# A selective-scan block on one core: delta*u stored twice and spread from sixteen rows, partitions in another order, two buffers for y

## The chip, the core and the metric

The kernel runs on one NeuronCore of a Trainium2 chip; the other cores are idle. The metric is the device time of one launch in microseconds (us). A core has five engines that run side by side and wait for each other through semaphores: PE (matmul), DVE (vector), ACT (activation), POOL (GpSimd) and SP, which here does nothing but issue DMA transfers. A transfer is cut into packets that run on up to 16 DMA engines[...].

## The reference, cut to what matters

Layer 0 is a residual block with a selective scan over 4 directions; layer 1 is linear attention and a feed-forward net in reduced precision. The change touches the scan and what feeds it.

```python
# xs: B=8 images, 4 directions k, 192 channels d, L = 64*64 positions
x_dbl = einsum('bkdl,kcd->bkcl', xs, x_proj_w)          # 6 + 16 + 16 rows
dts, Bs, Cs = split(x_dbl, [6, 22], axis=2)
delta = softplus(einsum('bkrl,kdr->bkdl', dts, dt_proj_w) + dt_proj_b)
A = -exp(A_log)                                         # 192 channels x 16 states
# for every position in turn:
h = exp(delta*A) * h + (delta*u) * B                    # [b, k, d, 16 states]
y = sum over states of h * C,  plus D*u
# then: sum of the 4 directions, layernorm, gate silu(z), projection, residual
x = x + ...
t = x + attention(layernorm(x));  t = t + ffn(layernorm(t))
```

## The kernel before, in words

The 8 images go through in 4 pairs, one pair after the other, and each pair through five stages: `front` (norms, input projection, depthwise convolution), `prepare`, `scan`, `back` (sum of the directions, norm, gate, projection) and `tail` (attention and feed-forward). Within `prepare`, `front`, `back` and `tail` the framework places the instructions; `scan` stands under `tc.manual_schedule()`, so that its instructions stand on each engine in the order in which the Python loop issues them. Every DMA of the kernel is issued on SP, in one queue. Eight semaphores are used for the DMAs in turn, so an issue can also wait until the transfer eight places ahead has landed.

`prepare` computes, per direction k and chunk of 512 positions, the rows B and C (L332 to L334, stored to the scratch tensors `bs` and `cs_`), delta (L341), and delta*u (L345). `spread` (L292) stores delta*u to the scratch tensor `du` (float32, pieces of 512 bytes) and delta, cut into three bf16 parts, to `dl` (pieces of 256 bytes).

`scan` works on 128 steps per pair: 4 directions times 32 time chunks of 128 positions (TC). The 128 partitions hold 16 states n and 8 slots s, where a slot is one of the 2 images b and one of 4 blocks of 48 channels; partition p = 8 n + s. The 48 channels of a block are walked in 4 rounds r of 12 channels (NI). Per step there are 8 half rounds v, two for each r:

- `fetch` (L432) loads `dut`: delta*u of one round, the same for all 16 states. It is one DMA of 128 rows of 6144 bytes, the source being 8 rows of `du` and a leading broadcast of 16:

```python
du[k, c, :, g % 4].rearrange("s i t -> s (i t)").unsqueeze(0).to_broadcast([NS, 8, NI * TC])
```

- `load` (L403) loads `dm`, delta in its three parts, for two rounds: 24 rows of 6144 bytes, each to 3 partitions. `decay` (L473) multiplies it on PE with `aw` (which holds A for each partition) and ACT takes the exponential (L491) in PSUM tile `da`.
- `drive` (L451): ACT copies the state carried over from the step before (L463), and POOL multiplies `dut` with B, tile `bt` (L466), into `dbu`.
- `run` (L493): DVE scans 6 channels times 128 positions (L501) from `da` and `dbu` into `h`.
- `sums` (L506): PE multiplies `h` with C, tile `cw` (L519), and ACT takes the result from PSUM to `yev` (L524). `yev` holds two steps and has one buffer; `store` (L529) writes it to `ys` after every second step with 4 DMAs, at v = 6.

`load_bc` (L416) is a generator that loads B and C for 4 steps at once: 4 DMAs for `bt` (32 partitions each, partitions j, j+4, ...), then 8 for `cw` (16 partitions each). `next(more)` (L556) issues one of these DMAs per v. Before the first step 4 of the 12 are issued (L545). `dut` has 4 buffers, `dm` 3, `bt`, `dbu` and `h` 2, `da` 3 and `yp` 2.

At the head of the kernel L91 to L101 load the projection weights with the two images' state columns interleaved, and L148 to L160 write the masked A to `awd` in the order (state, slot).

Of the kernel before, what the change touches and what calls it, by code (L numbers as in the profile page):

```python
# [10 lines left out]
F32 = mybir.dt.float32  # L11
# [25 lines left out]
W6 = 6 * SEG  # L37
HQ = TC // 4
LOGEXP = "natural_log_exp_and_others"

# [7 lines left out]
def vss_attn_ffn(ctx: ExitStack, tc: tile.TileContext, a: dict):  # L50
# [37 lines left out]

    xw = const.tile([128, KD, 3, 76], F32, name="xw")
    dtw = const.tile([128, KD, 3, 128], F32, name="dtw")  # L90
    with tc.tile_pool(name="xprep", bufs=2) as wp:  # L91
        for k in range(KD):
            for g in range(2):
                xg = wp.tile([128, 3, 2 * NS], F32, name="xg")
                nc.sync.dma_start(xg, a["xw"][k, :, g, :, 0:32])
                for b in range(2):
                    nc.vector.tensor_copy(
                        xw[:, k, :, 32 * g + b : 32 * g + 32 : 2], xg[:, :, NS * b : NS * b + NS]
                    )
            nc.sync.dma_start(xw[:, k, :, 64:76], a["xw"][k, :, 0, :, 32:44])  # L100
            nc.sync.dma_start(dtw[64:76, k], a["dtw"][k])  # L101

    def cut(name, v, *rest):

# [25 lines left out]
    with tc.tile_pool(name="aprep", bufs=1) as wp:  # L130
        am = wp.tile([128, KD, 2, NS], F32, name="am")
        nc.sync.dma_start(am, a["alog"])
        nc.scalar.activation(am, am, AF.Exp)
        nc.vector.tensor_scalar(am, am, -1.0, None, ALU.mult)
        for i in range(3):
            ap = wp.tile([128, KD, 2, NS], BF16, name=f"ap{i}")
            nc.vector.tensor_copy(ap, am)
            if i < 2:
                nc.vector.tensor_tensor(am, am, ap, ALU.subtract)
            for k in range(KD):  # L140
                nc.sync.dma_start(ad[i, k, 0:128], ap[:, k, 0])
                nc.sync.dma_start(ad[i, k, 128:DI], ap[0:64, k, 1])
        mask = wp.tile([72, 8], F32, name="mask")
        for p in range(3):
            nc.sync.dma_start(
                mask[24 * p : 24 * p + 24], ident[0:8, 0:8].unsqueeze(1).to_broadcast([8, 3, 8])
            )
        for k in range(KD):  # L148
            ac = wp.tile([72, 48 * NS], BF16, name="ac", bufs=2)
            for i in range(6):  # L150
                nc.sync.dma_start(
                    ac[12 * i : 12 * i + 12],
                    ad[:, k].rearrange("a (s c) n -> s a (c n)", s=4),
                )
            aw = wp.tile([72, 48 * NS, 8], BF16, name="awp", bufs=2)
            nc.vector.tensor_tensor(
                aw, ac.unsqueeze(2).to_broadcast([72, 48 * NS, 8]),
                mask.unsqueeze(1).to_broadcast([72, 48 * NS, 8]), ALU.mult,
            )
            nc.sync.dma_start(awd[k], aw.rearrange("p c m -> p (c m)"))  # L160


    w1q = const.tile([DIM, HID], F8, name="w1q")
# [137 lines left out]
    def prepare(xi, us, dl, du, bs, cs_):  # L301
        with ExitStack() as st:
            tmp = st.enter_context(tc.tile_pool(name="p2", bufs=3))
            ps = st.enter_context(tc.tile_pool(name="p2ps", bufs=3, space=PSUM))
            pd = st.enter_context(tc.tile_pool(name="p2pd", bufs=4, space=PSUM))

            for T in range(3):
                spread(lambda o, n: us[o : o + n], T, xi[T])
            dlv = dl.rearrange("k c a s r i t -> k c a (s r i) t")
            duv = du.rearrange("k c s r i t -> k c (s r i) t")  # L310
            for o in range(2):
                for c in range(NCH):
                    cs = bass.ts(c, F)
                    if o == 0:
                        u = [t[:, cs] for t in xi]
                    else:
                        u = []
                        for T in range(3):
                            ut = tmp.tile([128, F], F32, name=f"u{T}", bufs=2)
                            nc.gpsimd.tensor_copy(  # L320
                                ut.rearrange("p (w h) -> p w h", h=HH),
                                xi[T].rearrange("p (h w) -> p w h", w=HH)[:, bass.ts(c, ROWS), :],
                            )
                            u.append(ut)
                    for k in (o, o + 2):
                        pt = ps.tile([128, F], F32, name="pt")
                        for T in range(3):
                            nc.tensor.matmul(
                                pt[:76], xw[:, k, T], u[T], start=(T == 0), stop=(T == 2)
                            )  # L330
                        S = tmp.tile([128, F], F32, name="S")
                        nc.scalar.activation(S[:76], pt[:76], AF.Copy)  # L332
                        nc.sync.dma_start(bs[k, :, cs], S[0:32])
                        nc.sync.dma_start(cs_[k, :, cs], S[32:64])  # L334
                        for T in range(3):
                            pq = pd.tile([128, F], F32, name="pq")
                            nc.tensor.matmul(  # L337
                                pq, dtw[64:76, k, T], S[64:76], start=True, stop=True
                            )
                            d = tmp.tile([128, F], F32, name="delta")  # L340
                            nc.scalar.activation(  # L341
                                d, pq, AF.Softplus, bias=dtb[:, k, half(T) : half(T) + 1]
                            )
                            q = tmp.tile([128, F], F32, name="du")
                            nc.vector.tensor_tensor(q, d, u[T], ALU.mult)  # L345
                            j = slice(c * F // TC, (c + 1) * F // TC)
                            spread(
                                lambda o, n: duv[k, j, o : o + n].rearrange("j p t -> p j t"),
                                T, q.rearrange("p (j t) -> p j t", t=TC),
                            )  # L350

                            dp = tmp.tile([128, F // TC, 3, TC], BF16, name="dp")
                            rest = tmp.tile([128, F], F32, name="rest")
                            d, rest = [
                                t.rearrange("p (j t) -> p j t", t=TC) for t in (d, rest)
                            ]
                            nc.scalar.activation(dp[:, :, 0], d, AF.Copy)  # L357
                            nc.vector.tensor_tensor(rest, d, dp[:, :, 0], ALU.subtract)  # L358
                            nc.scalar.activation(dp[:, :, 1], rest, AF.Copy)  # L359
                            nc.gpsimd.tensor_tensor(dp[:, :, 2], rest, dp[:, :, 1], ALU.subtract)  # L360
                            spread(
                                lambda o, n: dlv[k, j, :, o : o + n]
                                .rearrange("j a p t -> p (j a) t"),
                                T, dp.rearrange("p j a t -> p (j a) t"),
                            )
            nc.scalar.preload_act_table_set(LOGEXP)


    def scan(dl, du, bs, cs_, ys):
        with ExitStack() as st:  # L370
# [45 lines left out]
            def load_bc(s):  # L416
# [6 lines left out]
                i = s // NB  # L423
                bt[i] = wk.tile([128, NB * TC], F32, name="bt")
                for j in range(4):
                    nc.sync.dma_start(bt[i][j::4], bs[k, :, ts])
                    yield
                for m in range(8):
                    nc.sync.dma_start(cw[i % 2][m::8, m, :], cs_[k, m // 4 :: 2, ts])
                    yield  # L430

            def fetch(g):  # L432
                if g >= 4 * N:
                    return
                k, c, _ = steps[g // 4]
                dut[g] = ring.tile([128, NI, TC], F32, name="dut")
                nc.sync.dma_start(
                    dut[g],
                    du[k, c, :, g % 4].rearrange("s i t -> s (i t)").unsqueeze(0)
                    .to_broadcast([NS, 8, NI * TC]),  # L440
                )

            def segs(t, back):
# [62 lines left out]
            def sums(s, f):  # L506

                if f == 0:
                    yev[s] = (
                        yev.pop(s - 1) if s % 2  # L510
                        else one.tile([128, 2, HQ, 48], F32, name="yev")
                    )
                h = hs[s][:, 1:, :].rearrange("p (i u) r -> p i u r", u=SEG)
                y = yp[f % 2]
# [27 lines left out]
            load(0)  # L542
            fetch(0)
            more = load_bc(0)
            for _ in range(4):  # L545
                next(more)
            for g in range(1, 3):
                load(g)
# [222 lines left out]
    for pair in range(npair):  # L771
        zs = dram.tile([2, 2, DIM, L], F32, name="zs")
        us = dram.tile([2 * DI, L], F32, name="us")
        dl = dram.tile([KD, NT, 3, 8, NR, NI, TC], BF16, name="dl")
        du = dram.tile([KD, NT, 8, NR, NI, TC], F32, name="du")
        bs = dram.tile([KD, 2 * NS, L], F32, name="bs")
        cs_ = dram.tile([KD, 2 * NS, L], F32, name="cs")
        ys = dram.tile([KD, 8, L, 48], F32, name="ys")
# [126 lines left out]
```

## Time and profile before

| what | us |
|---|---|
| median of 3 runs | 16007.57 (15930.12 to 16009.15) |
| the profiled execution, its own time | 16024.39 |
| its span, first to last instruction | 16022.1 |
| DVE scans L501, 4096 of 1758 ns | 7021.7 busy |
| POOL products L466, 2048 of 3445 ns | 7040.6 busy |
| ACT exponentials L491, 4096 of 798 ns | 3254.2 busy |
| PE matmuls L485 and L519 | 3242.8 and 3000.8 busy |

In the profile PE is a matmul, PEld a weight load, SPq the DMA-issuing queue. L466 is line 466 of the kernel. "busy" sums the durations of a group, "idle before" is the time in which the engine stood still just before an instruction of the group, with the releaser that ended it. The row DMA gives the mean busy share of the 16 DMA engines. A pair takes about 4000 us: the first scan instruction of the first pair stands at 748.3 us, and the second pair's first load at 4030 us.

### The profile page before, as it was taken

The numbers are of one execution on the slowest core, as the hardware profiler recorded it, in microseconds if no ns is written. First come the engines' busy times: TensorE is split into PE (matmuls) and PEld (weight loads), VectorE is DVE, ScalarE is ACT, GpSimd is POOL, SyncE is SP. The second block draws the span as 40 slices with busy tenths as digits, with TensorE's granted clock in tenths as the row PEclk, the third lists the DMA queues.
The fourth block names the chain that finished last, engine by engine and source line by source line (L and its number), as shares of the span: only waits on it lengthen the run. The fifth ranks groups of instructions, "written<-read, shape, count | busy, mean of one in ns | idle before, by whom it ended". The sixth has DMA issues, their size and how long they took to land. (4 is left out here: it accounts for less than half of the span.)

```text
span 16022.1 us, 390169 instructions
## 1 busy us (share of the span) xinstructions
PE 10317.2 (64%) x171008; PEld 6805.4 (42%) x171008; DVE 8452.8 (53%) x6351; ACT 6748.1 (42%) x11498; POOL 7760.5 (48%) x2682
## 2 busy tenths in 40 slices
PE   7755555567875555557787555555678755555577
PEld 2244444443324444444332444444533244444453
DVE  1466666642146666663214666666421466666632
ACT  2544444435354444443535444444353544444435
POOL 0466666620046666662004666666200466666620
PEclk9655555576865555557686555555778655555576
DMA  1999999971189999997119999999711999999971
GB/s 48 210 220 217 214 218 212 213 160 35 39 204 218 220 217 217 221 217 153 29 42 211 218 215 215 210 214 217 157 33 41 212 216 218 222 218 216 214 152 27
DMA packets 1903136, 2784.10 MB, mean 174 GB/s; under 512 B 1254372, under 2 KB 1451861, under 8 KB 1898837
## 3 DMA queue, kind: packets, MB, share of 16 engines
q1 hardware_dynamic: 1901428, 2759.13, 74.3%
q8 instruction: 1341, 21.97, 0.7%
q14 instruction: 367, 3.00, 0.1%
HBM read 2322.98 MB, written 435.63 MB: 172 GB/s over the span
## 5 line engine op out<-in xcount | busy, mean ns | idle before, releaser
L501 DVE TENSOR_TENSOR_SCAN h<-da,dbu 128x774 f32<-128x774 f32 x4096 | 7021.7, 1758 | 3454.8 <-POOL dbu L466 3364.1
L466 POOL TENSOR_TENSOR dbu<-dut,bt 128x1536 f32<-128x1536 f32 x2048 | 7040.6, 3445 | 3449.7 <-ACT dbu L463 1841.8
L485 PE MATMUL da<-dm,aw 72*128 72x128 bf16 (+2 forms) x28672 | 3242.8, 279 | 3868.9 <-DVE h L501 3522.9
L491 ACT ACTIVATE da<-da 128x768 f32<-128x768 f32 x4096 | 3254.2, 798 | 3503.1 <-PE da L485 3497.7
L485 PEld LDWEIGHTS <-aw 72*128 72x128 bf16 x28672 | 2500.7, 130 | 4452.9 <-issue 4364.7
L519 PE MATMUL yp<-h,cw 128*8 128x48 f32 x131072 | 3000.8, 272 | 752.5 <-issue 673.9
L519 PEld LDWEIGHTS yp<-h,cw 128*8 128x8 f32 x131072 | 2487.0, 122 | 1201.5 <-issue 1051.2
L524 ACT ACTIVATE yev<-yp 128x384 f32<-128x384 f32 x2048 | 1003.3, 490 | 2620.0 <-PE yp L519 1463.5
L320 POOL COPY u<-xi 128x512 f32<-128x512 f32 x96 | 111.4, 1175 | 1505.0 <-PE pc L283 1474.2
L360 POOL TENSOR_TENSOR dp<-rest,dp 128x512 bf16<-128x512 f32 x384 | 462.2, 1204 | 710.8 <-ACT dp L359 690.3
L283 PE MATMUL pc<-y,diag 128*128 128x512 f32 x1728 | 742.3, 592 | 0.0
L690 POOL MEMSET tn<- 1x4096 f32 x8 | 27.8, 3506 | 1384.4 <-DVE t L660 1384.4
L345 DVE TENSOR_TENSOR du<-delta,xi 128x512 f32<-128x512 f32 x192 | 131.9, 687 | 1066.7 <-ACT delta L341 779.7
L337 PE MATMUL pq<-S,dtw 12*128 12x512 f32 x768 | 580.8, 860 | 129.1 <-ACT delta L341 74.7
L358 DVE TENSOR_TENSOR rest<-delta,dp 128x512 f32<-128x512 f32 x384 | 302.5, 789 | 663.8 <-ACT dp L357 663.8
L760 POOL TENSOR_TENSOR ot<-t,y 96x512 f32<-96x512 f32 x64 | 73.5, 1149 | 1176.7 <-DVE y L758 1161.7
L623 PEld LDWEIGHTS py<-ident,yk 128*96 128x96 f32 x4096 | 521.3, 178 | 226.7 <-issue 192.0
L623 PE MATMUL py<-ident,yk 128*96 128x128 f32 x4096 | 544.5, 291 | 95.7 <-DMA yk<-ys 92.8
L283 PEld LDWEIGHTS pc<-y,diag 128*128 128x128 f32 x1728 | 326.4, 189 | 415.4 <-issue 415.4
L638 ACT ACTIVATE sq<-yc 96x512 f32<-96x512 f32 x128 | 75.9, 593 | 987.2 <-PE yc L635 882.7
L463 ACT COPY dbu<-h 128x12 f32<-128x12 f32 x1984 | 413.8, 209 | 37.4 <-DVE h L501 20.7
L337 PEld LDWEIGHTS pq<-S,dtw 12*128 12x128 f32 x768 | 156.5, 243 | 547.9 <-ACT delta L341 182.3
(125 smaller groups left out, 6894.5 us busy)
## 6 DMA issues: line engine op xcount, KB each, us to landing
dut<-du SPq DMA_DIRECT2D x2048, 768.0 KB
dm<-dl SPq DMA_DIRECT2D x1024, 432.0 KB
dl<-dp SPq DMA_DIRECT2D x256, 384.0 KB
ys<-yev SPq DMA_DIRECT2D x1024, 96.0 KB
du<-du SPq DMA_DIRECT2D x256, 256.0 KB
dl<-dp SPq DMA_DIRECT2D x256, 192.0 KB
yk<-ys SPq DMA_DIRECT2D x512, 96.0 KB
yk<-ys SPq DMA_DIRECT2D x1024, 48.0 KB
```

Of the source, the lines that this page charges most:

```text
L283: nc.tensor.matmul(pc, diag[:, half(T), t, :], pad[T][:, r0 + dy : r0 + dy + ROWS, dx : dx + HH], start=(t == 0), stop=(t == 8),)
L337: nc.tensor.matmul(pq, dtw[64:76, k, T], S[64:76], start=True, stop=True)
L358: nc.vector.tensor_tensor(rest, d, dp[:, :, 0], ALU.subtract)
L360: nc.gpsimd.tensor_tensor(dp[:, :, 2], rest, dp[:, :, 1], ALU.subtract)
L463: nc.scalar.copy(start, times(hs[s - 1][:, :, r])[:, :, 0 if back else TC - 1])
L466: nc.gpsimd.tensor_tensor(times(t), dut.pop(g), bt[s // NB][:, bass.ts(c % NB, TC)].unsqueeze(1) .to_broadcast([128, NI, TC]), ALU.mult,)
L485: nc.tensor.matmul(t[:, x0:x1], aw[k, r][:, 6 * hf + e, :], dm[p // 4][:, NI * (r % 2) + 6 * hf + e, x0 - lo : x1 - lo], start=True, stop= ...
L491: nc.scalar.activation(e, e, AF.Exp)
L501: nc.vector.tensor_tensor_scan(hs[s][:, w, r][:, d], da[p % 3][:, o : o + W6][:, d], dbu[4 * s + r][:, w][:, d], 0.0, ALU.mult, ALU.add,)
L519: nc.tensor.matmul(y[32 * q : 32 * q + 8, 48 * j : 48 * j + 48] .rearrange("p (r i) -> p i r", r=NR), cw[s // NB % 2][:, :, tb], h[:, :, t ...
L524: nc.scalar.activation(yev[s][:, steps[s][1] % 2, 8 * f : 8 * f + 8, :].rearrange("p j e -> p (j e)"), y[:, 0 : 8 * 48], AF.Copy,)
L623: nc.tensor.matmul(o, yk[:, k, j, g * DIM : (g + 1) * DIM], ident, start=(k + j == 0), stop=(k + j == KD + 2),)
```

## The change

delta*u is stored twice, to `du[k, c, v]` with v = 0 and 1. `fetch` reads 16 rows, (v s), each broadcast to 8 neighbouring partitions, in place of 8 rows under a broadcast of 16. The partitions are now ordered (half of the states v, slot s, state within the half): p = 64 v + 8 s + n. `bt` and `cw` follow: `bt` is filled by 4 DMAs of 32 partitions, each from 8 rows under a leading broadcast of 4; `cw` by 16 DMAs of 8 partitions in place of 8 of 16. 12 of the now 20 loads of `load_bc` are issued before the first step. `awd` is written in the new order, and the projection weights are loaded straight into their tile, without the interleaving copies on DVE. `yev` is taken from the pool with two buffers.

```diff
-    with tc.tile_pool(name="xprep", bufs=2) as wp:
-        for k in range(KD):
-            for g in range(2):
-                xg = wp.tile([128, 3, 2 * NS], F32, name="xg")
-                nc.sync.dma_start(xg, a["xw"][k, :, g, :, 0:32])
-                for b in range(2):
-                    nc.vector.tensor_copy(
-                        xw[:, k, :, 32 * g + b : 32 * g + 32 : 2], xg[:, :, NS * b : NS * b + NS]
-                    )
-            nc.sync.dma_start(xw[:, k, :, 64:76], a["xw"][k, :, 0, :, 32:44])
-            nc.sync.dma_start(dtw[64:76, k], a["dtw"][k])
+    for k in range(KD):
+        nc.sync.dma_start(xw[:, k, :, 0:32], a["xw"][k, :, 0, :, 0:32])
+        nc.sync.dma_start(xw[:, k, :, 32:64], a["xw"][k, :, 1, :, 0:32])
+        nc.sync.dma_start(xw[:, k, :, 64:76], a["xw"][k, :, 0, :, 32:44])
+        nc.sync.dma_start(dtw[64:76, k], a["dtw"][k])
...
-            aw = wp.tile([72, 48 * NS, 8], BF16, name="awp", bufs=2)
+            aw = wp.tile([72, 96, 8, 8], BF16, name="awp", bufs=2)
             nc.vector.tensor_tensor(
-                aw, ac.unsqueeze(2).to_broadcast([72, 48 * NS, 8]),
-                mask.unsqueeze(1).to_broadcast([72, 48 * NS, 8]), ALU.mult,
+                aw,
+                ac.rearrange("p (c n) -> p c n", n=8).unsqueeze(2).to_broadcast([72, 96, 8, 8]),
+                mask.unsqueeze(2).unsqueeze(1).to_broadcast([72, 96, 8, 8]), ALU.mult,
             )
...
-            duv = du.rearrange("k c s r i t -> k c (s r i) t")
+            duv = du.rearrange("k c v s r i t -> k c v (s r i) t")
...
-                            spread(
-                                lambda o, n: duv[k, j, o : o + n].rearrange("j p t -> p j t"),
-                                T, q.rearrange("p (j t) -> p j t", t=TC),
-                            )
+                            for v in range(2):
+                                spread(
+                                    lambda o, n: duv[k, j, v, o : o + n]
+                                    .rearrange("j p t -> p j t"),
+                                    T, q.rearrange("p (j t) -> p j t", t=TC),
+                                )
...
                 for j in range(4):
-                    nc.sync.dma_start(bt[i][j::4], bs[k, :, ts])
+                    v, b = divmod(j, 2)
+                    n0 = NS * b + 8 * v
+                    nc.sync.dma_start(
+                        bt[i][32 * j : 32 * j + 32],
+                        bs[k, n0 : n0 + 8, ts].unsqueeze(0).to_broadcast([4, 8, NB * TC]),
+                    )
                     yield
                 for m in range(8):
-                    nc.sync.dma_start(cw[i % 2][m::8, m, :], cs_[k, m // 4 :: 2, ts])
-                    yield
+                    for v in range(2):
+                        p0, n0 = 64 * v + 8 * m, NS * (m // 4) + 8 * v
+                        nc.sync.dma_start(
+                            cw[i % 2][p0 : p0 + 8, m, :], cs_[k, n0 : n0 + 8, ts]
+                        )
+                        yield
...
-                    du[k, c, :, g % 4].rearrange("s i t -> s (i t)").unsqueeze(0)
-                    .to_broadcast([NS, 8, NI * TC]),
+                    du[k, c, :, :, g % 4].rearrange("v s i t -> (v s) (i t)").unsqueeze(1)
+                    .to_broadcast([16, 8, NI * TC]),
...
-                        else one.tile([128, 2, HQ, 48], F32, name="yev")
+                        else wk.tile([128, 2, HQ, 48], F32, name="yev")
...
-            for _ in range(4):
+            for _ in range(12):
                 next(more)
...
-        du = dram.tile([KD, NT, 8, NR, NI, TC], F32, name="du")
+        du = dram.tile([KD, NT, 2, 8, NR, NI, TC], F32, name="du")
```

More of the change, by code (lines that the diff above doesn't have):

```diff
@@ L154, in vss_attn_ffn @@
                 )
-            aw = wp.tile([72, 48 * NS, 8], BF16, name="awp", bufs=2)
+            aw = wp.tile([72, 96, 8, 8], BF16, name="awp", bufs=2)
             nc.vector.tensor_tensor(
-                aw, ac.unsqueeze(2).to_broadcast([72, 48 * NS, 8]),
-                mask.unsqueeze(1).to_broadcast([72, 48 * NS, 8]), ALU.mult,
+                aw,
+                ac.rearrange("p (c n) -> p c n", n=8).unsqueeze(2).to_broadcast([72, 96, 8, 8]),
+                mask.unsqueeze(2).unsqueeze(1).to_broadcast([72, 96, 8, 8]), ALU.mult,
             )
-            nc.sync.dma_start(awd[k], aw.rearrange("p c m -> p (c m)"))
+            nc.sync.dma_start(awd[k], aw.rearrange("p c m n -> p (c m n)"))
     w1q = const.tile([DIM, HID], F8, name="w1q")
```

## The prediction

> **What bounds the kernel now.** I read the page first: span, slices, queues, costliest groups.
>
> ```profile
> span 16022.1 us, 390169 instructions
> ...
> DMA  1999999971189999997119999999711999999971
> GB/s 48 210 220 217 214 218 212 213 160 35 39 204 218 220 217 217 221 217 153 29 42 211 218 215 215 210 214 217 157 33 41 212 216 218 222 218 216 214 152 27
> ...
> L501 DVE TENSOR_TENSOR_SCAN h<-da,dbu 128x774 f32<-128x774 f32 x4096 | 7021.7, 1758 | 3454.8 <-POOL dbu L466 3364.1
> L466 POOL TENSOR_TENSOR dbu<-dut,bt 128x1536 f32<-128x1536 f32 x2048 | 7040.6, 3445 | 3449.7 <-ACT dbu L463 1841.8
> ...
> L524 ACT ACTIVATE yev<-yp 128x384 f32<-128x384 f32 x2048 | 1003.3, 490 | 2620.0 <-PE yp L519 1463.5
> ```
>
> In seven of ten slices of a pair the DMA engines are over 90% busy, yet move only about 217 GB/s; DVE and POOL, the busiest computing engines there, stand still a third of the time. Next come windows: two stages (prepare of the first pair, its scan) and two bare transfers, the store of `us` from 128 partitions and the load of the next input.
>
> ```profile
> 281.00:285.50 4.50, 4.50 (x12) 2.06 (x11) 0.00 (x0) 0.00 (x0) 0.00 (x0) 1.00 1.10 466
> 4031.50:4045.50 14.00, 0.00 (x0) 0.00 (x0) 14.00 (x19) 0.00 (x0) 10.27 (x3) 0.50 0.97 225
> 425.00:735.00 310.00, 245.49 (x344) 63.00 (x342) 141.03 (x191) 179.98 (x306) 131.54 (x112) 0.67 0.92 211
> 740.00:3360.00 2620.00, 1491.07 (x39609) 1236.30 (x39609) 1749.05 (x1021) 1095.16 (x2025) 1757.81 (x526) 0.55 0.93 216
> ```
>
> The last three columns are PE clock, DMA share and GB/s. Scan is 0.93 busy at 216 GB/s, prepare 0.92. The second row matters: a plain load, every row read once, runs at 225 GB/s with all engines busy, no faster than scan with its eight repeated rows. Last, the waits inside scan:
>
> ```profile
> DVE h L501 <- POOL dbu L466: 847.6, 406, 7.9
> POOL dbu L466 <- ACT dbu L463: 470.8, 188, 7.0
> POOL dbu L466 <- DMA dut<-du: 351.4, 203, 4.9
> ACT yev L524 <- DMA ys<-yev: 277.5, 57, 8.0
> ```
>
> DVE waits for POOL, and POOL for `dut` or for ACT. Whether DMA is the bound is settled by the trace's landing records (the semaphore increments of each transfer). From 760 to 3330 us a `dut` lands a median 13.7 us after its issue, a `dm` 12.8, and the slowest DMA engines always have a backlog: the gaps between successive last landings sum to the whole stretch, `dut` 502 times 3.37 us, `dm` 251 times 2.45, `ys` 248 times 0.51, `cw` 0.31 and `bt` 0.34 each. A `dut` is 8 packets of 6144 bytes on each of 16 engines, so 421 ns a packet; the shortest such packets take 234. A step lasts 20.43 us; POOL alone would need 4 x 3.445 = 13.8, DVE 8 x 1.758 = 14.1. So DMA bounds scan, and a gain there could reach nearly a third before DVE holds it.
>
> [...]`dm` (24 rows to 72 partitions) lands on 12 engines, `ys` (8) on 8, `dut` on 16.[...]
>
> **The change part by part.**
>
> *dut from 16 rows.* Same packets, same engines and partitions; only which row an engine reads is new. 2048 x 3.37 us = 6.90 ms hang on it. No row shows it, so I bound it. Below: no gain, since the plain load, with distinct rows, runs at 225. Nearest likeness: `dm`[...]. With 12 engines in `dm` and 4 in `dut` the trace moves 245 GB/s, with all 16 in `dut` 233: 5% more. Above: sorting moments with only `dut` in flight by the number of different rows being read (the engines drift apart, so it is 2 to 12 already, most often 6) gives 215 GB/s at two, 231 at six, 252 at ten, some 5 GB/s per row; sixteen would give about 275, 17% shorter. Drift and rows come together, so this is an upper guide. Floor: 234 ns, 44% shorter. I take 7%: 0.07 x 6.90 ms = -483 us; ends +345 (5% worse[...]) and -1170.
>
> *bt and cw.* A group of four steps has 4 `bt` and 8 `cw`. Engines 0 to 3 now take all of `bt`: 8 packets of 2 KB at 145 ns, 1.2 us in place of 0.33, 4 x 0.87 = 3.5 us. `cw` becomes 16 transfers on engines 0 to 7: 8 more at 0.30 = 2.4 us. [...]engines 0 to 3 gain 5.9 us on 81.7, 7%. Unrelieved: 128 groups x 5.9 = 755 us. Relief: an engine moves 14.6 GB/s when 16 are active, 16.0 when 12 are. I take 450; ends 0 (one shared capacity) and 755. SP has eight more issues of about 0.5 us per 82 us, and waits less than it can spare. All 20 are issued before the fourth step ends; `cw` is needed only in the step after: no new wait. They also take places among the eight DMA semaphores; steps with `cw` loads (19.7 and 20.9 us) are no longer than those without (20.0 and 21.2), so I add nothing.
>
> *du twice.* Prepare of a pair holds 49,094 packets of 512 bytes at 31.6 ns, 97 us over 16 engines, and with `dl` (179 us) and the rest 291 us of DMA in 320. Twice `du` makes 388. What is free, 26 us, hides part: +68 if all is filled, +97 if the packing stays, with a little over for SP[...]. I take +85, times 4 pairs = +340; ends 270 and 420. Behind the doubled stores stand `dl` stores on SP, and ACT L357 waits for their buffer: that is how it shows.
>
> *Second yev.* L524 waits 1042.2 us in all for `ys` to land, 217 times, and behind it on ACT stand the carry copies L463 for which POOL waits. It would pay if ACT were the bound. But DMA works off its backlog meanwhile: 8 to 12 us after a store it moves 230 to 249 GB/s, above the mean. What is late next is `dut`. I take 0; end -300 (odd steps, with the store, are 1.2 us longer, 256 times).
>
> *Small.* Eight more `cw` issues ahead of the second `dut` at each scan start: 4 x 5 = +20. The 16 copies L97 (904 ns) go, off the path; the `awp` products (4 of 6546 ns) change shape beside PE's work. 0.
>
> Sum: -483 + 450 + 340 + 0 + 20 = +327 on a span of 16,022.1, 16,349; the execution's own time lies 2 us above its span, the median of runs 17 us below it. I say 16,340.
>
> **Rivals.** *The rows lift the pace (faster).* One mechanism: engines that read the same row at the same time queue at the memory. At -17%, 15,650; it decides from -12% on, where it outweighs the 810 us of cost. At the floor DVE would hold a step at some 15.5 us: about 13,850. For it, the trend by rows; against it, the plain load and `dm`. *The rows do nothing, engines 0 to 3 count in full:* 16,022 + 755 + 340 + 20 = 17,140, and with half the relief 16,950. For it, that reads seem to go at one pace whatever is read; against it, the pace rises with fewer engines active. *The second y buffer pays its 300 us:* with the forecast's other terms 16,050, no change. *The change doesn't do what it says:* the new `dut` may split over engines otherwise than one row each; then it is the second rival.
>
> **How the numbers follow.** Forecast 0.42 (own range 16,120 to 16,650), rows do nothing 0.24, no change 0.08, rows lift the pace 0.26. A difference within 0.5% can't be told from no change here. Faster 0.26, same 0.08, slower 0.66. The range takes the trend's 15,650 and somewhat beyond, to 15,300, and stops at 17,050.
>
> **What would show it.** Prepare longer by 70 to 100 us a pair. In scan, `dut` packets near 390 ns, DMA share falling below 0.93 as engines 4 to 15 wait for 0 to 3. L524's wait for `ys` gone and the step no shorter for it. I am wrong if `dut` packets fall below 350 ns (POOL and DVE then idle less), or if the step shrinks with packets unchanged: then ACT's stall was the bound.

## The result, and the profile after

The changed kernel takes 16,737.6 us (median of 4 runs, 16,729.66 to 16,747.25) against 15,976.72 us beside it: 761 us longer, a ratio of 1.0479 (95% interval 1.0445 to 1.0512). The forecast was 16,340, some 330 us longer.

These are lines of the page of the changed kernel; L509 is the scan (L501 before), L474 the POOL product (L466), L532 the ACT copy to `yev` (L524).

```profile
span 16745.1 us, 392110 instructions
...
DMA  2988888871199888887119888898712988888871
GB/s 60 225 208 204 208 207 209 209 162 39 49 226 209 209 208 207 209 204 161 38 50 225 207 206 209 210 209 205 161 37 55 225 210 207 208 208 209 207 157 33
...
L509 DVE TENSOR_TENSOR_SCAN h<-da,dbu 128x774 f32<-128x774 f32 x4096 | 7023.4, 1758 | 3945.8 <-POOL dbu L474 3862.4
L474 POOL TENSOR_TENSOR dbu<-dut,bt 128x1536 f32<-128x1536 f32 x2048 | 7041.8, 3444 | 3884.3 <-DMA dut<-du 3076.0
...
L532 ACT ACTIVATE yev<-yp 128x384 f32<-128x384 f32 x2048 | 1005.7, 491 | 1860.3 <-PE yp L527 1834.8
```

Busy times and means are those of before. What grew is idle time: DVE ahead of its scans by 491 us (3454.8 to 3945.8), POOL ahead of its products by 435 us (3449.7 to 3884.3). In the scan slices the DMA engines are less busy (8 in place of 9) and move some 208 GB/s in place of 217. Windows of the changed kernel: prepare of the first pair and its scan (last columns: PE clock, DMA share, GB/s).

```profile
425.00:820.00 395.00, 234.67 (x339) 62.51 (x338) 170.81 (x184) 177.15 (x294) 133.55 (x108) 0.64 0.96 226
850.00:3560.00 2710.00, 1510.27 (x39859) 1250.15 (x39858) 1740.49 (x1016) 1124.16 (x2019) 1744.09 (x519) 0.55 0.89 206
```

Prepare runs at 0.96 busy, scan at 0.89 where it had 0.93. And the waits within that scan:

```profile
DVE h L509 <- POOL dbu L474: 931.9, 425, 6.7
POOL dbu L474 <- DMA dut<-du: 757.8, 340, 6.7
ACT yev L532 <- PE yp L527: 444.8, 490, 7.4
...
POOL dbu L474 <- ACT dbu L471: 95.0, 46, 6.0
```

ACT's wait for `ys`, 277.5 us in this stage before, is down to 3.8, and POOL's wait for ACT has shrunk from 470.8 to 95.0. In their place POOL waits for `dut`: 757.8 us where it was 351.4.

By stage, from the trace: prepare (first to last softplus) took 306, 322, 306 and 309 us in the four pairs and now takes 392, 391, 391 and 392, together 323 more. Scan (first to last DVE scan) took 2618, 2589, 2630 and 2599 and now takes 2720, 2721, 2716 and 2714, together 435 more. The other stages together came out 35 us shorter (the span grew by 723, from 16,022.1). A step went from 20.43 to 21.29 us. The semaphore steps of the landings, read as one for each DMA engine, count the engines of a transfer: a `dut` still lands in 16 steps, a `bt` in 4 and a `cw` in 8, where both had 16 (with 4, 8 or 12 there is one step more, in the median 0.5 to 1.3 us after the issue, where the next comes at 5.5 or later). This is the split that the prediction counted on. Its names, engines 0 to 3 and 0 to 7, stand for these 4 and 8; the trace does not number the engines, and that the 4 are among the 8 that carry `cw` and `ys` (8 steps) was my estimate.

### The profile page after: what moved, and what is told of

It is laid out like the page before. It is cut to its first block, busy times and chain, and to the rows that moved or that the text cites. A ratio compares the mean times of both kernels' runs of the same rounds, so it can differ in the third digit from the quotient of the medians.

```text
span 16745.1 us, 392110 instructions
## 1 busy us (share of the span) xinstructions
PE 10316.5 (62%) x171008; PEld 6843.3 (41%) x171008; DVE 8569.9 (51%) x6335; ACT 6893.9 (41%) x11498; POOL 7786.6 (47%) x2682
## 5 line engine op out<-in xcount | busy, mean ns | idle before, releaser
L509 DVE TENSOR_TENSOR_SCAN h<-da,dbu 128x774 f32<-128x774 f32 x4096 | 7023.4, 1758 | 3945.8 <-POOL dbu L474 3862.4
L474 POOL TENSOR_TENSOR dbu<-dut,bt 128x1536 f32<-128x1536 f32 x2048 | 7041.8, 3444 | 3884.3 <-DMA dut<-du 3076.0
L493 PE MATMUL da<-dm,aw 72*128 72x128 bf16 (+2 forms) x28672 | 3282.3, 280 | 4423.4 <-DVE h L509 4080.0
L527 PEld LDWEIGHTS yp<-h,cw 128*8 128x8 f32 x131072 | 2521.6, 124 | 1056.8 <-issue 972.7
L532 ACT ACTIVATE yev<-yp 128x384 f32<-128x384 f32 x2048 | 1005.7, 491 | 1860.3 <-PE yp L527 1834.8
L359 POOL TENSOR_TENSOR dp<-rest,dp 128x512 bf16<-128x512 f32 x384 | 496.2, 1293 | 1043.2 <-ACT dp L358 1043.2
L341 DVE TENSOR_TENSOR du<-delta,xi 128x512 f32<-128x512 f32 x192 | 201.9, 1051 | 1176.5 <-ACT delta L337 773.5
```

Of the source, the lines that this page charges most:

```text
L474: nc.gpsimd.tensor_tensor(times(t), dut.pop(g), bt[s // NB][:, bass.ts(c % NB, TC)].unsqueeze(1) .to_broadcast([128, NI, TC]), ALU.mult,)
L493: nc.tensor.matmul(t[:, x0:x1], aw[k, r][:, 6 * hf + e, :], dm[p // 4][:, NI * (r % 2) + 6 * hf + e, x0 - lo : x1 - lo], start=True, stop= ...
L509: nc.vector.tensor_tensor_scan(hs[s][:, w, r][:, d], da[p % 3][:, o : o + W6][:, d], dbu[4 * s + r][:, w][:, d], 0.0, ALU.mult, ALU.add,)
L527: nc.tensor.matmul(y[32 * q : 32 * q + 8, 48 * j : 48 * j + 48] .rearrange("p (r i) -> p i r", r=NR), cw[s // NB % 2][:, :, tb], h[:, :, t ...
L532: nc.scalar.activation(yev[s][:, steps[s][1] % 2, 8 * f : 8 * f + 8, :].rearrange("p j e -> p (j e)"), y[:, 0 : 8 * 48], AF.Copy,)
```

## The experiments

The prediction had scan as good as unchanged (-483 for `dut`, +450 for `bt` and `cw`, +20 at the start). The trace after showed the gap up to a `dut`'s last landing (from the landing of the transfer issued before it, as in the prediction) at 3.42 us, where it had been 3.37: the gain was missing. Why could different rows not help? Theory 1: reads go at one pace, whatever is read. Theory 2: engines that read the same row at the same time queue for it, so other rows lift the pace. Theory 3: what slows `dut` is the form of the transfer, how its rows are handed over to the partitions, whatever rows it reads. The first two kernels set them against each other. In the code shown, lines with + stand where the lines with - stood; code without - lines stands for the same source of `dut` as the first, or for its whole transfer. Kernels that read other rows than the reference compute other values, but move as many bytes.

**Sixteen rows alone** (on the kernel before; du is stored once):

```
-  du[k, c, :, g % 4].rearrange("s i t -> s (i t)").unsqueeze(0).to_broadcast([NS, 8, NI * TC])
+  du[k, c - c % 2 : c - c % 2 + 2, :, g % 4].rearrange("c s i t -> (c s) (i t)")
+      .unsqueeze(1).to_broadcast([16, 8, NI * TC])
```

> The kernel before, with dut alone read from 16 different rows 24 KB apart, each broadcast to 8 neighbouring partitions, as in the kernel after; delta*u is stored once, so the second 8 rows are those of the neighbouring chunk (the values are not the reference's; bytes, packets and waits are the same). Theory 1, one read pace whatever rows are read: a dut stays at 3.3 to 3.45 us on the slowest engines, and the time within 1% of before, 15,900 to 16,150. Theory 2, rows lift the pace and other parts of the change eat it: dut near 2.8 to 3.1, time 14,850 to 15,500. Theory 3, the bound is where the packets land[...]: same as theory 1.

Measured: 15,967.57 us, ratio 0.9981 (0.9968 to 0.9993). From its page:

```profile
GB/s 48 210 215 214 214 217 217 214 163 40 37 202 218 218 216 221 215 219 158 36 36 212 221 215 215 216 213 216 161 34 40 212 219 213 223 219 214 220 153 28
...
L467 POOL TENSOR_TENSOR dbu<-dut,bt 128x1536 f32<-128x1536 f32 x2048 | 7037.8, 3443 | 3433.8 <-ACT dbu L464 1870.1
```

A `dut` lands every 3.43 us, a step takes 20.40, and POOL stands idle as long as before. Sixteen rows, 24 KB apart as in the change, are worth 0.2%: theory 2 falls, and with it the step of the forecast that counted on it.

**128 plain rows, no broadcast:**

```
-  du[k, c, :, g % 4].rearrange("s i t -> s (i t)").unsqueeze(0).to_broadcast([NS, 8, NI * TC])
+  du[k, c - c % 4 : c - c % 4 + 4].rearrange("c s r i t -> (c s r) (i t)")
```

> The kernel before, with dut read as 128 different rows of 6 KB that lie one behind the other, one row to each partition, no broadcast (the values are not the reference's; as many bytes and packets as before). Theory 1, one pace of some 225 GB/s for every read from memory: a dut stays near 3.4 us, time within 2% of before. Theory 3, what holds a dut is how its broadcast spreads over partitions and engines: without the broadcast a dut falls to 1.9 to 2.4 us, POOL and DVE become the bound, time 13,700 to 14,600. Theory 2 (repeated reads of one row queue up): as theory 3, or somewhat slower, under 15,000.

Measured: 14,679.01 us, ratio 0.9171 (0.9151 to 0.9192), with as many bytes in as many packets. From its page:

```profile
span 14683.5 us, 390169 instructions
...
GB/s 53 194 243 249 246 247 247 245 153 30 40 182 248 245 250 252 243 247 156 30 40 183 247 249 249 248 254 248 150 24 38 204 245 246 249 251 250 247 145 18
...
L465 POOL TENSOR_TENSOR dbu<-dut,bt 128x1536 f32<-128x1536 f32 x2048 | 7024.4, 3447 | 2156.3 <-ACT dbu L462 1847.2
```

Scan moves some 248 GB/s in place of 217, POOL's idle time falls by 1293 us (3449.7 to 2156.3), a step takes 17.86 us, a `dut` lands every 2.71 us. So reads do not go at one pace, and theory 1 falls. Theory 3 had promised somewhat more, 13,700 to 14,600 us and a `dut` of 1.9 to 2.4. Two things differ from the kernel before, though: no row is read twice, and the transfer has another form. A fourth theory stood beside the third: repeated reads of one row are slow. The next two kernels part them.

**128 different rows, but in 16 groups of 8:**

```
+  du[k, c - c % 8 : c - c % 8 + 8].rearrange("c s r i t -> (c s r) (i t)")
+      .rearrange("(o n) x -> o n x", n=16)[:, :8, :]
```

> The kernel before with dut read from 128 different rows, as in the run with 128 plain rows, but handed over as 16 groups of 8 rows with a gap between the groups[...]. No row is read twice. It computes with the wrong delta*u. Theory 3[...]: dut stays near 3.4 us, the time within 1% of 16,000. Theory 4 (what is slow is reading the same row many times): as with plain rows, dut 2.7 us, 14,600 to 14,800.

**One row, read 128 times:**

```
+  du[k, c, 0, g % 4].rearrange("i t -> (i t)").unsqueeze(0).to_broadcast([128, NI * TC])
```

> The kernel before with dut as one single row of du broadcast to all 128 partitions. It computes with the wrong delta*u. One row is read 128 times, and the transfer has 128 equal rows on both sides, as the plain one. Theory 3 (the partitions written): as with 128 plain rows, 14,600 to 14,900, dut 2.7 us. Theory 4 (repeated reads): at least as slow as before, 16,000 or more, dut 3.4 us or more.

Measured: the groups take 15,950.51 us, ratio 0.9977 (0.9965 to 0.999), `dut` 3.32; the single row takes 14,689.07 us, ratio 0.9191 (0.9166 to 0.9215), `dut` 2.67. Each page's rates, and POOL; first the 16 groups, then the single row:

```profile
GB/s 49 210 218 217 220 222 212 216 159 34 37 214 219 217 214 219 219 220 155 33 41 212 217 215 220 216 221 217 158 30 38 213 223 219 216 222 218 216 155 28
...
L466 POOL TENSOR_TENSOR dbu<-dut,bt 128x1536 f32<-128x1536 f32 x2048 | 7039.0, 3444 | 3375.0 <-ACT dbu L463 1904.6
```

```profile
GB/s 53 198 250 247 246 246 249 245 147 22 38 203 249 247 251 249 241 248 145 18 38 205 247 247 250 240 248 245 146 22 38 210 242 248 248 250 245 245 144 18
...
L466 POOL TENSOR_TENSOR dbu<-dut,bt 128x1536 f32<-128x1536 f32 x2048 | 7025.1, 3447 | 2181.4 <-ACT dbu L463 1840.9
```

Both times it is as theory 3 has it. 128 different rows in 16 groups of 8 are as slow as the broadcast; one row read 128 times is as fast as 128 rows. Neither the number of rows nor reading them again matters here, only the form in which the transfer is handed over: 16 groups of 8 (15,951 us) against 128 equal rows (14,679 and 14,689). Why the form counts is not shown: no trace tells which engine writes which partition. The packets say the same. Of those of 6144 bytes in the scan of the first pair (`dut` and `dm`, 800 to 3000 us), 10% last under 260 ns before the change, after it, and with the groups, with medians of 421, 428 and 418 ns; with 128 plain rows it is 47% (median 273), with one row 45% (282). And 248 GB/s is a mean over all transfers of the scan. At moments with all 16 engines in a `dut`, an estimate that matches engines to transfers by their landings gives 233 GB/s before, 236 with the groups, 336 with plain rows and 315 with one row.

**Interleaved transfers.** If the form is what counts, another form for the same data may pay. The data of the kernel before, in its partitions, fetched by several interleaved transfers in place of one; four transfers, then two:

```
+  for b in range(4):          # in the second kernel 2, with b::2 and a broadcast to [NS, 4, ...]
+      nc.sync.dma_start(dut[g][b::4],
+          du[k, c, b::4, g % 4].rearrange("s i t -> s (i t)").unsqueeze(0)
+          .to_broadcast([NS, 2, NI * TC]))
```

In the expectations "alternation" is this interleaving. Of the first, 3.2 us and 15,700 are for the case that it helps, 15,950 to 16,150 for the case that it does not.

> The kernel before, with each dut loaded by 4 transfers of 32 partitions (b, b+4, b+8, ...) from 2 rows of du under a broadcast of 16, in place of one of 128. [...]the result is the same. Theory 3[...] dut falls below 3.2 us and the time below 15,700. [...]15,950 to 16,150, or more, since 12 more issues a step take up SP and the eight semaphores.

> The same with 2 transfers of 64 partitions (b, b+2, ...) from 4 rows[...]. If alternation helps: less than with four transfers, 15,500 to 15,900. If not: 15,950 to 16,100.

Measured: four transfers 15,525.83 us, ratio 0.9714 (0.9685 to 0.9743); two transfers 15,388.67 us, ratio 0.9637 (0.9603 to 0.967). From the page of two:

```profile
GB/s 50 211 229 231 227 230 229 228 156 30 37 207 230 231 228 232 233 230 154 27 37 214 232 231 231 230 229 232 150 24 37 217 232 232 230 232 230 226 149 23
...
L467 POOL TENSOR_TENSOR dbu<-dut,bt 128x1536 f32<-128x1536 f32 x2048 | 7039.9, 3445 | 2835.5 <-ACT dbu L464 1659.0
```

A `dut` now lands in two parts of 1.56 us, 3.12 together; in four parts of 0.73, 2.92 together. The median packet falls from 421 to 385 and 320 ns. So the same bytes, to the same partitions, go faster when only their order and grouping change; the cause is not shown. Four came out as forecast, two below their range, and my ranking failed: four land a `dut` sooner, but take longer in all. The page of four shows a longer wait of ACT for `ys`, 1395.8 us in place of 877.4 with two and 1042.2 before.

```profile
L525 ACT ACTIVATE yev<-yp 128x384 f32<-128x384 f32 x2048 | 1002.2, 489 | 2335.9 <-DMA ys<-yev 1395.8
```

Every fourth step takes 24.05 us there. The trace points at the number of issues. From 800 to 3100 us SP spends 84% of the time inside issue instructions, against 55% with two transfers and 36% before; after the step that also loads `cw`, the store goes out only 3.1 us into the next step, the long one, while the other store of the four steps goes out 15.3 us into its own. The DMA engines, at 0.93 busy in the scan before, are at 0.82. The eight semaphores are the less likely cause: SP waits for landings for 206 us of this stretch, where it had waited for 629 before. What stays open is whether the order, or the cutting into two by itself, makes the gain of two: two transfers that don't interleave were not run.

**The second y buffer alone:**

```
-  else one.tile([128, 2, HQ, 48], F32, name="yev")
+  else wk.tile([128, 2, HQ, 48], F32, name="yev")
```

> The kernel before with the second yev buffer alone. My forecast: L524's wait for ys goes (1042 us in all), the time stays within 0.5% of before, since the DMA backlog sets the step. Rival: ACT's stall counts in full, 300 us less, about 15,680.

Measured: 16,006.62 us, ratio 1.0005 (0.9991 to 1.002). Its page shows the stall change its name:

```profile
L466 POOL TENSOR_TENSOR dbu<-dut,bt 128x1536 f32<-128x1536 f32 x2048 | 7038.0, 3443 | 3371.1 <-DMA dut<-du 2323.2
...
L524 ACT ACTIVATE yev<-yp 128x384 f32<-128x384 f32 x2048 | 1003.8, 490 | 2100.3 <-PE yp L519 2069.6
```

Before, ACT was named for 1841.8 of POOL's 3449.7 us of idle time; now `dut` is, for 2323.2 of 3371.1. With the interleaved `dut` the same was tried again:

> The kernel before with dut in two interleaved transfers, as the last run (15,389), and with the second buffer for y. If a DMA backlog still sets the step there, the second buffer again gives nothing: 15,340 to 15,440. If ACT's waits for ys to land (219 us in the first pair's scan of the last run) begin to cost time once dut is shorter: 15,100 to 15,300.

Measured: 15,349.97 us, ratio 0.9602 (0.956 to 0.9643), against 0.9637 (0.9603 to 0.967) without: the intervals overlap, and nothing is shown for it there either. From its page, POOL again:

```profile
L467 POOL TENSOR_TENSOR dbu<-dut,bt 128x1536 f32<-128x1536 f32 x2048 | 7046.2, 3447 | 2774.7 <-DMA dut<-du 1760.7
```

**Taking the change down part by part.** First `bt`, in the changed kernel, from 32 different rows without the leading broadcast (the arguments of the transfer are shown; B lands in partitions that no longer fit the new order):

```
-  bt[i][32 * j : 32 * j + 32], bs[k, n0 : n0 + 8, ts].unsqueeze(0).to_broadcast([4, 8, NB * TC])
+  bt[i][32 * j : 32 * j + 32], bs[k, :, ts]
```

> The kernel after, with each bt DMA read from 32 different rows to its 32 partitions, without the leading broadcast of 4, so that it can spread over 16 engines (the values of B are then not the reference's). If engines 0 to 3, which carry all of bt, set the pace: 3.5 us less per four steps, 450 us at most, 200 or more expected: 16,290 to 16,540. If what counts is the bytes in all: no change, 16,690 to 16,780.

Then `cw` too, as the 8 transfers of before, with 4 issued ahead of the first step:

```
-  for v in range(2):
-      ...
-      nc.sync.dma_start(cw[i % 2][p0 : p0 + 8, m, :], cs_[k, n0 : n0 + 8, ts])
-      yield
+  nc.sync.dma_start(cw[i % 2][m::8, m, :], cs_[k, m // 4 :: 2, ts])
+  yield
```

> The changed kernel with bt from 32 rows on all 16 engines and also cw as 8 transfers of 16 partitions on 16 engines, as before the change, with 4 issued ahead of the first step. B and C land in partitions that no longer fit the new order, so the values are wrong. Left of the change are delta*u stored twice, dut from 16 rows, and the second y buffer. If the extra cost of scan is bt and cw alone: 16,260 to 16,380, which is before plus the longer prepare, with a step of 20.4 us. If dut from the doubled du has a cost of its own: 16,420 or more, as with bt alone put back.

And from the other side, the kernel before with nothing but the second store:

```
-  spread(lambda o, n: duv[k, j, o : o + n]..., T, q...)
+  for v in range(2):
+      spread(lambda o, n: duv[k, j, v, o : o + n]..., T, q...)
```

> The kernel before with delta*u stored twice, and only the first copy read; all else unchanged. Forecast +340 (270 to 420), and the profiles' prepare stages give +324: 16,270 to 16,380, prepare 390 us a pair, a step 20.4 us. If the doubled du slows its readers too (rows lie twice as far from one chunk to the next), the step is longer and the time above 16,420.

| kernel | us | ratio to before (95%) | step, us |
|---|---|---|---|
| before + second store | 16,334.97 | 1.0219 (1.0189 to 1.0249) | |
| changed, `bt` and `cw` as before | 16,300.32 | 1.0195 (1.0169 to 1.022) | 20.35 |
| changed, `bt` as before | 16,477.80 | 1.0300 (1.027 to 1.033) | 20.71 |
| changed | 16,737.60 | 1.0479 (1.0445 to 1.0512) | 21.29 |

By the ratios and a time before of 15,980 us, read downwards: the second store +350 us, `dut` from 16 rows with the second y buffer and the small changes at the head -38, which the intervals do not tell from nothing, `cw` with its earlier issues +168, `bt` +286; by the medians the last two are 177 and 260. Together that is 766, for 761 by the medians. With both put back, scan is as before: rates from the page of the second kernel of the table,

```profile
GB/s 57 226 213 218 219 215 219 218 162 32 50 227 219 217 222 211 217 220 157 31 54 226 215 218 216 218 214 216 157 30 48 227 218 215 218 218 218 219 156 29
```

217 GB/s in scan, and still 226 or 227 in the prepare slices, which the doubled stores lengthen.

## Why the prediction was wrong

*What bounds the kernel: right,* but not the reach of "nearly a third". A shorter `dut` alone, with nothing else touched, took 8% off the time. At a step of 17.86 us DVE is not yet the limit (14.1): with 128 plain rows POOL's wait for `dut` is down from 1425.9 to 198.5 us, and its wait for ACT's carry copy stands at 1847.2, as before (1841.8). That wait was not in the estimate.

*dut from 16 rows, -483: the step that failed.* It measured -0.2% alone (some -30 us), so some 450 us of gain in the sum were not there; the miss was 761 - 332 = 429. Three readings led there. First, the trend by rows (215 GB/s at two rows, 252 at ten) was taken for an effect of the rows, though drift came with them. That the rows do not make it is shown. It also appears, by an estimate from the landings, with the 16 groups, where no row is read twice: some 230 GB/s where the engines stand at three different places of their eight packets, 243 at eight. Both estimates take each engine to work through its eight packets in order, which no trace shows, and what makes the trend is not shown either. Second, `dm` was taken for a likeness of other rows, when it also lands in 12 steps in place of 16 and fills 72 partitions in place of 128. Third, the bound from below: the plain load at 225 GB/s was read as "no faster than scan", a pace of reading. That load fills 96 partitions with rows of 16 KB (`xt`, L207), so it is no likeness of 128 equal rows; with these the scan itself ran at 248. A transfer's likeness is its form on both sides, and I looked at the source alone.

*bt and cw, +450, and +20 at the start: right.* The runs give 168 + 286 = 454 for the two parts, the start included; the first step of a scan went from 19.2 to 23.0 us, 15 us in four pairs. `bt` lands every 0.78 us in place of 0.34, for which 1.2 in place of 0.33 was the unrelieved figure; `cw` every 0.26 in place of 0.31, but twice as often. The DMA share fell from 0.93 to 0.89, as was to be expected if the other engines wait for the four of `bt`; which of them wait the trace does not tell. The relief of 0.6 was a choice between ends; that the sum came within 20 us is in part luck.

*du twice, +340: right.* 323 us in the stages of prepare, 350 alone by the ratio (interval 302 to 398). The +85 a pair were 81 in `prepare`, and some 7 more passed between its last softplus and the first scan (33 us before, 40 with the second store alone). ACT's wait for the `dl` stores shows it, as said: 67.8 us before, 423.1 after.

*Second yev, 0: right,* and in the way given: what is late next is `dut`. The kernel with that buffer alone shows the exchange: POOL's wait for ACT fell from 1841.8 to 716.5 us, that for `dut` rose from 1425.9 to 2323.2.

*Rivals.* Of the ways it could go, "the rows do nothing" is what happened, but with the forecast's own price for `bt` and `cw`, not with the full 755 or half of the relief: 16,022 + 450 + 340 + 20 = 16,832, against 16,738. (Two slips of the working changed nothing here: half the relief is 602, so 16,985 in place of 16,950, and 291 us of DMA in 320 leave 29 free, not 26.) "The rows lift the pace" is refuted by the sixteen rows alone, "the second y buffer pays" by that buffer alone.

*What would show it.* Prepare longer by 70 to 100 us a pair, the DMA share below 0.93 and the wait for `ys` gone with no shorter step: all three came. `dut` packets near 390 ns did not: the median of the 6144-byte packets went from 421 to 428. Neither of the two signs of being wrong came, packets below 350 ns or a shorter step: they watched for a gain larger than forecast, not for one that fails to come.

## What to carry to other kernels

Where a broadcast load is the bound, ask in which form it is handed over, as equal rows or as groups, before asking which rows it reads: with 16 groups of 8 this scan ran at 217 GB/s, with 128 equal rows at 248, whether these were one row or 128. If the data do not allow 128 equal rows, try the same load as two interleaved transfers, which took 3.6% off the kernel before the change and beats both versions; with four, 2.9% were left, and SP spent 84% of the time from 800 to 3100 us inside issue instructions, against 55% with two. And a small load under a leading broadcast of 4 was dear here, out of proportion to its bytes: the four `bt` of 64 KB per four steps cost about 270 us in all (260 by the medians, 286 by the ratios), landing in 4 steps in place of 16 and every 0.78 us in place of 0.34. The reading that fits is the prediction's, that everything waits for the four engines that carry them; the runs show the cost, not who waits.

## What the runs showed that I had not expected

- Reading one row 128 times costs nothing that shows: 14,689 us against 14,679 with 128 different rows.
- The kernel could be 8% faster by the form of `dut` alone; a step would then be 17.9 us. Even so the median packet of 273 ns stands above the shortest, some 234, and 128 equal rows still land every 2.7 us where eight packets of 234 ns would need 1.9. The DMA engines are less busy there (0.87 in that scan, where it was 0.93), which I take for a part of it; the rest is open.
- POOL's two waits, for ACT and for `dut`, hide each other. The second y buffer shortened the first and left POOL's idle time at 3371 us, of 3450; 128 plain rows shortened the second and left the wait for ACT as it was. Both together, with 128 equal rows, were not run; with two interleaved transfers the second buffer showed nothing.
